# First states copied by ACT, half of the mixed differences on ACT and GpSimd, lower halves of the values subtracted from PSUM, in a two-layer RWKV kernel

## The chip, the cores and the metric

The kernel runs on one core of a Trainium2 chip. The metric is the device time of one execution in microseconds (us); lower is better. One execution was profiled.

Engines are called PE (the tensor engine; PEld is its weight load), DVE (VectorE), ACT (ScalarE), POOL (GpSimd) and SP (SyncE, which here only issues DMAs). Each works through its own instructions in order. SBUF is the working memory; PSUM is the memory that PE writes its products to, in banks of 512 float32 a partition.

## The reference, cut to what matters

The program is four layers one after the other on `x` of 16 sequences x 100 steps x 512 channels: an attention layer (0), an RWKV layer (1), an attention layer with a feed-forward part (2), and an RWKV layer (3) of the same form as layer 1. The change touches the RWKV layers alone. What one of them computes, shortened:

```python
xa = ln(x); sx = previous_step(xa) - xa                       # differences between steps
xxx = tanh((xa + sx * maa_x) @ maa_w1)                        # then five products with maa_w2
xm = xa[:, :, None] + sx[:, :, None] * (maa_stack + xxx)      # five mixes: k, w, v, r, g
w = exp(-exp(time_decay + tanh(xw @ td_w1) @ td_w2))
r, k, v = xr @ Wr.T, xk @ Wk.T, xv @ Wv.T;  g = silu(xg @ Wg.T)
def step(s, rkvw):                                            # 32 heads, state 16 x 16 each
    a = k[..., :, None] * v[..., None, :]
    out = einsum('bhi,bhij->bhj', r, u * a + s)
    return a + w[..., :, None] * s, out
out = group_norm(scan(step, s0, (r, k, v, w)))
x1 = x + (out * g) @ Wo.T
# then a channel part: layer norm, two mixes, Wfk, Wfr, Wfv
```

The state at the start, `s0`, comes from the context tensor.

## The kernel before

One RWKV layer is the function `rwkv(n, ...)`. The 16 sequences are taken in four groups `g` of four; a group's tiles hold 128 channels x `T` = 400 columns (4 sequences x 100 steps). The 512 channels are four chunks `c`; over the four groups there are 16 chunks `C`.

**Units.** The recurrence of one chunk is cut into 8 units of two value columns each, so a layer has `UNITS` = 128 units `u`. A unit needs `w` and `k` of its chunk, and the values `v` of two columns spread over the partitions:

- `spread(u)`: two PE matmuls write the spread values into `vbs[u % 2]`, one of two PSUM tiles of two banks each, shifted by one column. The values go through the PE as two float32r halves, `hi` and `lo` (`lo` = value minus `hi`), which `split` makes and which pass through DRAM and come back as the chunk's tile `xc`.
- `product(u)`: a DVE copy (128 x 8 elements) puts the first states, from `first_states[g]`, into the first column of each sequence, and a DVE product multiplies the other columns by `k` in place.
- `scan(u)`: two DVE scans over 400 columns make the states `a`; POOL multiplies them by `r`.
- `gather(p)`: for two units at once, PE sums the products into the PSUM bank `acc`. After a chunk's last one, `norm(C)` makes the group norm: ACT copies and squares, and two slots later `variance` takes one PE matmul, then an Ln and an Exp on ACT, each with a load of its function table.

**Slots.** The main loop runs over slots `u`. In each slot it calls `spread(u + 1)`, `product(u)`, `slots.begin()` (work put off to this slot, `variance` among it), `scan(u)`, `slots.end()` (late readers of PSUM banks), then the transfers and small steps of the chunk, and `gather` in every second slot. Then it fills the slot with `pieces`: the projections and mixes of a coming group, output products and the channel part of a finished one, each with a cost in us, until 2.85 us or a little less is used up.

**Banks.** The pieces use three PSUM banks in turn, `slots.bank()`. A reader that is put off with `slots.read_later(bank, fn)` is written at the end of the next slot, or earlier if its bank is wanted again.

**Mixes.** `mixed(fs, c)` makes one or two of the five products with `maa_w2` for chunk `c`. Its reader `read` is one DVE instruction, (product + `maa_stack`) x `sx`, from PSUM into a tile `tm` (a ring of four that other steps use too), and one POOL sum with `xa` into `xj[f]`, which the projections of `linear` read.

**Values.** `plain(2, "Wv", "v", co)` reads a value projection: ACT copies the bank to `v` and stores it, `split` makes `hi` on ACT from the bank, and, put off with `read_later`, `lo` on DVE from the tile `v` in SBUF and `hi`.

Every DVE, ACT, POOL and PE instruction of these steps is kept in the order in which the program text issues it (`InOrder`, whose line L89 most rows of the profile bear; PE's is L94). DMAs issued by SP are placed by the scheduler. Group 0's projections run before unit 0, at negative slots; the projections of groups 1 to 3 run beside the units.

Of the kernel before, what the change touches and what calls it, by code (L numbers as in the profile page):

```python
# [10 lines left out]
F32R = mybir.dt.float32r  # L11
BF16 = mybir.dt.bfloat16
U8 = mybir.dt.uint8
AF = mybir.ActivationFunctionType
ALU = mybir.AluOpType
# [3 lines left out]
NC = E // 128  # L19
G = 4  # L20
NG = B // G
T = G * L
# [15 lines left out]
def xattn_sequence(ctx: ExitStack, tc: tile.TileContext, d: dict, out: bass.AP):  # L38
# [52 lines left out]
    vector, scalar, gpsimd = InOrder(nc.vector), InOrder(nc.scalar), InOrder(nc.gpsimd)  # L91

    def mm(**kw):
        pin(nc.tensor.matmul(**kw))  # L94
# [606 lines left out]
    def rwkv(n, ws, small, first, next_weights, last):  # L701
# [6 lines left out]
        with ExitStack() as es:  # L708
# [9 lines left out]
            vec, w1, td1, gwb = (small[k] for k in ("vec", "w1", "td1", "gwb"))  # L718
# [29 lines left out]
            put, first_states, lower = {}, {}, {}  # L748
# [170 lines left out]
            def states(g):  # L919

                s0 = first_states[g] = two.tile([128, NC, G, 16], F32, tag="s0", name=f"s0_{n}_{g}")
                nc.sync.dma_start(out=s0, in_=d["s0"][:, :, g * G : (g + 1) * G, :])

            def projections(g, base):
# [6 lines left out]
                def store(t, c, tile):  # L931
                    (nc.sync if t in ("lo", "g") else scalar).dma_start(out=to[t][c], in_=tile)

                rows = [xb[g * G + i] for i in range(G)]
                st, xn, xj = {}, [], {}
# [85 lines left out]
                def mixed(fs, c):  # L1021

                    banks = []
                    for f in fs:
                        if c == 0:
                            xj[f] = two.tile([128, NC, T], F32, tag="xm", bufs=4, name=f"xj_{nm}_{f}")
                        banks.append(slots.bank())
                    for f, ps in zip(fs, banks):
                        cols = slice(c * 128, (c + 1) * 128)
                        mm(out=ps[:, :T], lhsT=w2[f][:, cols], rhs=zs[f], start=True, stop=True)  # L1030

                    def read(f, ps):
                        tm = two.tile([128, T], F32, tag="tm", bufs=4, name=f"tm_{nm}_{f}_{c}")
                        vector.scalar_tensor_tensor(
                            tm, ps[:, :T], vec[f"stack{f}"][:, c : c + 1], st["sx"][:, c, :], ALU.add, ALU.mult
                        )
                        gpsimd.tensor_tensor(steps(xj[f][:, c, :]), steps(tm), xa(c), ALU.add)

                    for f, ps in zip(fs, banks):
                        mixes[f].append(slots.read_later(ps, lambda f=f, ps=ps: read(f, ps)))  # L1040
# [10 lines left out]
                def plain(f, w, t, co):  # L1051
                    def read(ps):
                        out = stage(f"{t}_{nm}_{co}")
                        scalar.copy(out[:, :T], ps[:, :T])
                        store(t, co, out[:, :T])
                        if t == "v":
                            split(ps, out[:, :T])

                    def split(ps, v):

                        hi = stage(f"hi_{nm}_{co}")[:, :T]
                        scalar.copy(hi.bitcast(F32R), ps[:, :T])
                        store("hi", co, hi)

                        lo = stage(f"lo_{nm}_{co}")[:, :T]

                        def low():
                            vector.tensor_tensor(lo.bitcast(F32R), v, hi, ALU.subtract)
                            store("lo", co, lo)

                        lows[co] = slots.read_later(ps, low)

                    linear(f, ws[w], co, read, ("in", g, co if t == "r" else 0))
# [259 lines left out]
            vb4 = lambda u: vbs[u % 2][:, :, 1 : T + 1].rearrange("p i (b t) -> p i b t", t=L)  # L1333

            def spread(u):

                C, j = u // 8, 2 * (u % 8)
                for i in range(2):
# [2 lines left out]
                        start=True, stop=True,  # L1341
                    )

            def product(u):
                C, j = u // 8, 2 * (u % 8)
                g = C // NC
                vector.tensor_copy(
                    vb4(u)[:, :, :, 0], first_states[g][:, C % NC, :, j : j + 2].rearrange("p b i -> p i b")
                )
                p4 = vb4(u)[:, :, :, 1:L]  # L1350
                vector.tensor_tensor(
                    p4, p4,
                    steps(chunks[u // 8]["k"])[:, None, :, 0 : L - 1].to_broadcast([128, 2, G, L - 1]), ALU.mult,
                )
# [78 lines left out]
            UNITS, LEAD = 32 * NG, (36.0, 46.0, 42.0)  # L1433
            START = -19
            u, due, blended = START, 0.0, 0
            while u < UNITS + 6 or pieces or slots.due or slots.late:
                slots.now = u
                if u == UNITS + 2 and not last:
                    nws[""] = first_stats(f"a{n}", vector, gpsimd)
                if u == UNITS:  # L1440
                    for i in range(max(len(pieces) - 8, 0), len(pieces)):
                        pieces[i] = (pieces[i][0], u + 9, *pieces[i][2:])
                if u % 32 == 0 and 0 < u <= UNITS:
                    output(u // 32 - 1, u + 7)
                short = sum(p[0] for p in pieces) < LEAD[(len(put) == NG) + (blended > 0)]
                for g in range(NG):
                    if u == max(32 * g - 24, START):
                        states(g)
                    if u == max(32 * g - 4, START + 6):
                        centered(first_states[g].rearrange("p c b s -> p (c b) s"), 16, f"s{n}_{g}")  # L1450
                if u == START + 3:
                    centered(ws["Wv"].rearrange("p c (x s) -> p (c x) s", s=16), 128, f"w{n}")
                if u == START + 10:
                    ws["Wo"] = load_turned(d[f"L{n}_Wo"], f"l{n}_Wo")
                if u == START:
                    projections(0, u + 1)
                elif short and u > START + 10 and len(put) < NG:
                    wait = int(left(("mix", len(put) - 1, 4)) / 2.6) + 2
                    projections(len(put), u + (max(wait, 9) if u > 0 else 6))
                elif short and len(put) == NG and blended < NG:  # L1460
                    g = blended
                    if u >= 32 * g + 40 and not any(p[3] == ("wo", g) for p in pieces):
                        if g == 0:
                            cm.update(load(n, "Wfk", "Wfr", "Wfv"))
                        wait = max(int(left() / 2.6) - 5, int(left(("mix", NG - 1, 4)) / 2.6) + 1, int(left(("keys", g - 1)) / 2.6)) if u < UNITS else 0
                        channel_stream(g, u + max(wait, (3, 3, 3, 2)[g]), (1, 1, 1, 0)[g])
                        blended += 1
                if u >= UNITS and set(nws) <= {""} and not any(p[3] == ("wo", NG - 1) for p in pieces):
                    nws.update(next_weights())
                unit = 0 <= u < UNITS  # L1470
                if 0 <= u + 1 < UNITS:
                    spread(u + 1)
                if unit:
                    product(u)
                slots.begin()
                if unit:
                    scan(u)
                slots.end()
                C, at = u // 8 + 1, u % 8
                if 0 <= C < NC * NG:  # L1480
                    if at == 2:
                        enter(C)
                    elif at == 6:
                        bonus(C, 0)
                C = u // 8
                if 0 <= C < NC * NG and at == 0:
                    bonus(C, 1)
                if 0 <= C < NC * NG and at == 2:
                    bonus(C, 2)
                if 0 < C <= NC * NG and at == 4:  # L1490
                    gates(C - 1)
                if u % 2 and 0 <= (u - 3) // 2 < UNITS // 2:
                    gather((u - 3) // 2)

                due = min(due, 0.0) + (2.85 if 0 <= u < UNITS else 3.9)
                due -= 0.45 * (u % 2) + 0.7 * (at in (0, 2, 3)) if unit else 0.0
                for p in [p for p in pieces if p[0] == 0 and not callable(p[1]) and p[1] <= u]:
                    take(p)
                while due > 0:
                    p = following(u)  # L1500
                    if p is None:
                        break
                    due -= take(p)
                u += 1
# [360 lines left out]
    def load(layer, *names):  # L1865
        return {k: load_w(d[f"L{layer}_{k}"], f"l{layer}_{k}") for k in names}
# [80 lines left out]
```

## Time and profile before

| | us |
|---|---|
| median of 3 runs | 3128.99 (3123.95 to 3131.28) |
| profiled execution, its time | 3127.86 |
| profiled execution, its span | 3126.1 |

| engine | busy in the span, us | share | instructions |
|---|---|---|---|
| PE | 2858.8 | 91% | 16323 |
| DVE | 1675.5 | 54% | 3507 |
| ACT | 1308.6 | 42% | 2921 |
| POOL | 1159.3 | 37% | 953 |

The profile gives, for one execution, the busy time of each engine, also in 40 equal slices of the span (each digit is a share in tenths) and in any window; the granted clock of PE (`PEclk`, 1.00 is full); groups of instructions of one line, engine, operation and tile (`out<-in`, shapes, `x`count, then busy us, mean ns of one, then the engine's idle time just before them and what ended it); the waits (who waited for whom: us in total, times, longest us); a timeline (start us, duration us); and the chain of work that ended last. Buffer numbers are left out of tile names: `mm` is any of the three banks, `vb` either of the two spread tiles.

### The profile page before, as it was taken

The page shows a single profiled execution, that of the slowest core. Times are in us where ns is not written, and L with a number is a line of the kernel's source. Part 1 is how long each engine was busy: PE and PEld are TensorE (multiplying, and loading weights), DVE is VectorE, ACT ScalarE, POOL GpSimd, SP SyncE. Part 2 cuts the span into 40 slices and gives each one's busy share as a digit, 9 for nine tenths or more (in the row PEclk, how much of TensorE's full clock was granted, in tenths as well). Part 3 has the DMA queues.
Part 4 walks back from the last instruction along what each step waited for, and adds up shares of the span by engine and source line. Part 5 has one row for each costly group of instructions (what it writes and reads, how often), then busy time and mean ns, then how long its engine had stood idle before and what let it go on. Part 6 is the DMA issues. An engine that isn't in the chain of part 4 may idle for free. (4 is left out here: it accounts for less than half of the span.)

```text
span 3126.1 us, 44079 instructions
## 1 busy us (share of the span) xinstructions
PE 2858.8 (91%) x16323; PEld 1488.0 (48%) x16323; DVE 1675.5 (54%) x3507; ACT 1308.6 (42%) x2921; POOL 1159.3 (37%) x953
## 2 busy tenths in 40 slices
PE   6999999878889999989999999989999789999998
PEld 3555555534344444444555555455555344444444
DVE  2555556553989988433333333331000369998981
ACT  3777677753435355422222232221111335344553
POOL 0111111133777777412222111220000367787771
PEclk9999999989999999989999999999999889999999
DMA  6010101013224353230000001020002323324321
GB/s 196 24 34 24 34 24 37 3 39 116 80 77 129 96 161 87 71 88 21 21 22 21 21 21 34 28 71 11 11 11 62 101 63 106 109 76 155 105 60 56
DMA packets 139561, 195.93 MB, mean 63 GB/s; under 512 B 23974, under 2 KB 106854, under 8 KB 139346
## 3 DMA queue, kind: packets, MB, share of 16 engines
q1 hardware_dynamic: 116306, 160.34, 17.3%
q10 hardware_dynamic: 23040, 32.78, 2.9%
q8 instruction: 128, 2.10, 0.3%
q14 instruction: 87, 0.71, 0.1%
HBM read 117.16 MB, written 49.15 MB: 53 GB/s over the span
## 5 line engine op out<-in xcount | busy, mean ns | idle before, releaser
L89 POOL TENSOR_TENSOR a<-a,rc 128x800 f32<-128x800 f32 x256 | 487.8, 1908 | 175.8 <-DVE a L89 113.1
L89 DVE TENSOR_TENSOR_SCAN a<-wc,vb 128x400 f32<-128x400 f32 x512 | 477.4, 974 | 28.1 <-PE acc L94 2.2
L89 DVE CUSTOM_DVE_ANT_0 pr<-l_sc,mask 100x361 f32<-100x361 f32 x512 | 252.1, 529 | 148.7 <-PE l_sc L94 148.6
L89 ACT ACTIVATE pr<-pr,nm 100x361 f32<-100x361 f32 x512 | 301.2, 593 | 5.8 <-POOL sums L89 3.7
L89 DVE TENSOR_TENSOR vb<-vb,kc 128x792 f32<-128x792 f32 x256 | 253.8, 991 | 8.8
L97 PEld LDWEIGHTS l_pT<-ident,pr 100*121 100x121 f32 x1536 | 193.3, 186 | 104.3 <-issue 50.9
L1639 DVE CUSTOM_DVE_ANT_0 junk<-l2a_sc,mask 100x361 f32<-100x361 f32 x256 | 136.9, 535 | 182.5 <-PE l2a_sc L94 165.0
L94 PE MATMUL vb<-xc,sel 128*128 128x400 f32 x512 | 207.0, 487 | 18.0 <-DVE a L89 17.8
L97 PE MATMUL l_pT<-ident,pr 100*121 100x100 f32 x1536 | 216.4, 276 | 6.2 <-ACT pt L89 4.3
L1675 POOL TENSOR_TENSOR pa<-pt,pt 121x1600 f32<-121x1600 f32 x16 | 57.1, 3570 | 363.7 <-ACT pt L1670 363.7
L89 ACT COPY pt<-l_pT 121x400 f32<-121x400 f32 x256 | 125.1, 489 | 149.5 <-PE l_pT L97 148.5
L1860 DVE TENSOR_TENSOR x<-pb,x 100x512 f32<-100x512 f32 x16 | 12.6, 790 | 319.9 <-DMA pb<-po 310.1
L89 POOL TENSOR_TENSOR xj<-tm,ext 128x400 f32<-128x400 f32 x160 | 153.6, 981 | 80.1 <-DVE tm L89 59.8
L94 PE MATMUL v<-l_v_w,ct 128*121 128x512 f32 x384 | 177.0, 605 | 0.0
L75 PE MATMUL h<-yTb,l_fc 128*128 128x400 f32 x512 | 172.8, 499 | 0.6 <-ACT yTb L343 0.6
L94 PE MATMUL k<-ct,l_k_w 128*128 128x361 f32 x512 | 170.6, 476 | 0.0
L75 PE MATMUL p<-l_proj,h 128*128 128x512 f32 x384 | 165.5, 592 | 0.0
L89 POOL TENSOR_SCALAR ve<-mv 100x1 f32<-100x1 f32 x16 | 3.6, 224 | 409.8 <-DVE mv L89 409.8
L94 PEld LDWEIGHTS vb<-xc,sel 128*128 128x128 f32 x512 | 97.2, 198 | 109.5 <-issue 36.1
L94 PE MATMUL l_sc<-kz,qz 32*100 32x361 f32 x1024 | 112.6, 509 | 36.1 <-DVE nm L89 33.9
L89 DVE COPY pt<-l_pT 121x400 f32<-121x400 f32 x128 | 73.5, 574 | 132.1 <-PE l_pT L97 64.8
L75 PEld LDWEIGHTS h<-yTb,l_fc 128*128 128x128 f32 x512 | 96.9, 190 | 74.3 <-ACT yTb L343 2.5
(298 smaller groups left out, 5158.0 us busy)
## 6 DMA issues: line engine op xcount, KB each, us to landing
ct<-in_ctxT SPq DMA_DIRECT2D x32, 722.0 KB
dk<-k ACTq DMA_DIRECT2D x32, 200.0 KB
kc<-dk SPq DMA_DIRECT2D x32, 200.0 KB
dv<-v ACTq DMA_DIRECT2D x32, 200.0 KB
dhi<-hi ACTq DMA_DIRECT2D x32, 200.0 KB
dlo<-lo SPq DMA_DIRECT2D x32, 200.0 KB
vc<-dv SPq DMA_DIRECT2D x32, 200.0 KB
dw<-wd ACTq DMA_DIRECT2D x32, 200.0 KB
```

Of the source, the lines that this page charges most:

```text
L75: nc.tensor.matmul(out=ps, lhsT=lhs(c), rhs=rhs(c), start=(c == 0), stop=(c == n - 1))
L89: return lambda *args, **kw: tc.keep_in_program_order(op(*args, **kw))
L94: pin(nc.tensor.matmul(**kw))
L97: pin(nc.tensor.transpose(out, in_, ident))
L1639: nc.vector.tensor_tensor_reduce(out=junk, in0=ss[r][:L, :S2], in1=t["mask"], scale=-1.0, scalar=FLT_MAX, op0=ALU.add, op1=ALU.min, accum_ ...
L1675: nc.gpsimd.tensor_tensor(t["pa"], t["pt"][0], pt, ALU.add)
L1860: nc.vector.tensor_tensor(x, pb[:, i, :], x, ALU.add)
```

## The change

Three edits, all inside `rwkv`:

1. The copy of the first states leaves `product(u)` and DVE. A new function `begin_states(u)` does it on ACT, and the main loop calls it for unit u + 1 in slot u, after `slots.begin()`.
2. In `mixed`, for groups 1 to 3 and where f + c is odd, the one DVE instruction becomes an ACT activate (product + `maa_stack`, from PSUM into `tm`) and a POOL product with `sx` in place. That is 10 of the 20 mixes of a group, 30 of the 80 of a layer.
3. `lo` is subtracted from the PSUM bank instead of from the copy `v` in SBUF; it stays on DVE and stays put off.

```diff
                     def read(f, ps):
                         tm = two.tile([128, T], F32, tag="tm", bufs=4, name=f"tm_{nm}_{f}_{c}")
-                        vector.scalar_tensor_tensor(
-                            tm, ps[:, :T], vec[f"stack{f}"][:, c : c + 1], st["sx"][:, c, :], ALU.add, ALU.mult
-                        )
+                        if (f + c) % 2 and g:
+                            scalar.activation(tm, ps[:, :T], AF.Identity, bias=vec[f"stack{f}"][:, c : c + 1], scale=1.0)
+                            gpsimd.tensor_tensor(tm, tm, st["sx"][:, c, :], ALU.mult)
+                        else:
+                            vector.scalar_tensor_tensor(
+                                tm, ps[:, :T], vec[f"stack{f}"][:, c : c + 1], st["sx"][:, c, :], ALU.add, ALU.mult
+                            )
                         gpsimd.tensor_tensor(steps(xj[f][:, c, :]), steps(tm), xa(c), ALU.add)
...
-                            split(ps, out[:, :T])
+                            split(ps)
...
                         def low():
-                            vector.tensor_tensor(lo.bitcast(F32R), v, hi, ALU.subtract)
+                            vector.tensor_tensor(lo.bitcast(F32R), ps[:, :T], hi, ALU.subtract)
                             store("lo", co, lo)
...
+            def begin_states(u):
+
+                C, j = u // 8, 2 * (u % 8)
+                scalar.copy(
+                    vb4(u)[:, :, :, 0], first_states[C // NC][:, C % NC, :, j : j + 2].rearrange("p b i -> p i b")
+                )
+
             def product(u):
-                C, j = u // 8, 2 * (u % 8)
-                g = C // NC
-                vector.tensor_copy(
-                    vb4(u)[:, :, :, 0], first_states[g][:, C % NC, :, j : j + 2].rearrange("p b i -> p i b")
-                )
                 p4 = vb4(u)[:, :, :, 1:L]
                 vector.tensor_tensor(
...
                 if unit:
                     product(u)
                 slots.begin()
+                if 0 <= u + 1 < UNITS:
+                    begin_states(u + 1)
                 if unit:
                     scan(u)
                 slots.end()
```

In the built program the instructions of PE stand in the same order before and after.

More of the change, by code (lines that the diff above doesn't have):

```diff
@@ L1056, in read, with split @@
                         if t == "v":
-                            split(ps, out[:, :T])
-                    def split(ps, v):
+                            split(ps)
+                    def split(ps):
                         hi = stage(f"hi_{nm}_{co}")[:, :T]
```

## The prediction

> **What bounds the kernel now.** I read the page's 40 slices first, since the change touches only the two RWKV layers.
>
> ```profile
> PE   6999999878889999989999999989999789999998
> DVE  2555556553989988433333333331000369998981
> ACT  3777677753435355422222232221111335344553
> POOL 0111111133777777412222111220000367787771
> ```
>
> VectorE (DVE) is at 80 to 90% in two stretches alone, slices 11 to 16 and 34 to 39 (counted from 1): the 128 units of layer 1 and of layer 3. There the tensor engine (PE) is as full, while ACT has room. The table of busy time for the two stretches (the second is a near copy of the first):
>
> ```profile
> core 0: us, PE busy (x) PEld busy (x) DVE busy (x) ACT busy (x) POOL busy (x), PEclk, DMA share, GB/s
> 780.00:1290.00 510.00, 466.87 (x2058) 226.45 (x2058) 454.33 (x642) 232.04 (x416) 393.18 (x306) 0.96 0.33 100
> 2530.00:3045.00 515.00, 474.92 (x2076) 230.22 (x2077) 456.30 (x643) 232.30 (x417) 396.73 (x306) 0.94 0.31 96
> ```
>
> Per unit 4.0 us: DVE 3.55, PE 3.65, POOL 3.1, ACT 1.8. So PE has 43 us idle in the first stretch and 40 in the second. Beyond that only a fuller clock could help (0.96 and 0.94 granted). What DVE does there, by groups of the first stretch:
>
> ```profile
> L89 DVE TENSOR_TENSOR_SCAN a<-wc,vb 128x400 f32<-128x400 f32 x248 | 231.2, 974 | 14.5 <-PE acc L94 1.6 <-DVE vb L89 1.0 <-POOL a L89 0.9
> L89 DVE SCALAR_TENSOR_TENSOR tm<-mm,vec,sx 128x400 f32<-128x400 f32 x60 | 35.3, 620 | 5.9 <-PE mm L94 4.4 <-POOL xj L89 1.2
> L89 DVE COPY vb<-s 128x8 f32<-128x8 f32 x124 | 20.2, 163 | 19.0 <-PE vb L94 19.0
> L89 DVE TENSOR_TENSOR lo<-v,hi 128x400 fp32r<-128x400 f32 x12 | 16.3, 1354 | 3.6 <-ACT hi L89 3.3
> ```
>
> The last three rows are what the change touches. DVE waits for PE before the copies only 19 us in all, so most units are set by DVE. The waits between 800 and 1260 us say the same from PE's side (its weight load and its matmul wait for the reader of a PSUM bank):
>
> ```profile
> PEld mm L94 <- DVE tm L89: 21.5, 21, 2.2
> PE mm L94 <- DVE tm L89: 8.7, 10, 1.8
> ```
>
> **First states.** Removed from DVE: 256 copies of 0.163 us, 0.20 us from the copy's start to the product's: 128 x 0.20 = 25.6 us a layer. Added to ACT: as many 8-element copies. No row shows one; the nearest are ACT's accumulator reads (187 ns) and its 128x128 activate (268 ns): I take 0.2, between 0.16 (DVE's own) and 0.27. On ACT, with 278 us free in a stretch, 26 us of work is hidden. [...]
>
> The price is the wait. DVE's product of unit u+1 now waits for ACT's copy, and ACT works in order: the copy stands behind all that slot u's begin puts on ACT. Once in 8 units that is the group norm's Ln and Exp with two table loads:
>
> ```profile
> 1079.62 1.28 ACT L89 ACT_TABLE_LOAD   x1 [5.07 <-PE mm L94]
> 1080.92 0.59 ACT L89 ACTIVATE sq<-mm,eps 128x400 f32<-128x400 f32 x1
> 1081.53 1.28 ACT L89 ACT_TABLE_LOAD   x1
> 1082.82 0.54 ACT L89 ACTIVATE sq<-sq 128x400 f32<-128x400 f32 x1
> ```
> ```profile
> 1078.76 1.86 DVE L89 TENSOR_TENSOR_SCAN a<-wc,vb 128x400 f32<-128x400 f32 x2
> 1080.54 0.15 DVE L89 COPY vb<-s 128x8 f32<-128x8 f32 x1
> 1080.73 0.99 DVE L89 TENSOR_TENSOR vb<-vb,kc 128x792 f32<-128x792 f32 x1
> ```
>
> Here DVE copied at 1080.54; ACT is free at 1083.36, so with 0.3 us for copy and signal the product starts 2.9 us later than now, and behind it on DVE stand two scans and the bank readers (ox here) that PE waits for. I did this for all units: the end of the ACT instruction that stands ahead of the new copy (or of the spread's matmul, if later) plus 0.3 us, less the start of DVE's copy now. In layer 1 the 14 Ln/Exp slots are late by 38 us in sum: 20 in units 0 to 89, 18.5 in units 90 to 127. In 44 other slots it is late by 40 us in sum, mostly by under 1 us and where DVE waits for PE's spread anyway; the exceptions are the value projections, where ACT itself is full (1100 to 1120 us: up to 4 us late). Units 0 to 89 are set by DVE: I charge all 20. In units 90 to 127 PE is the fuller one (10.0 of 10 us in most windows) and the second vb buffer gives DVE a unit of slack: I charge a third, 6. Of the 40 I charge a quarter, 10. All of it charged would be 78, none 0: kept for the range.
>
> **Mixed differences.** In groups 1 to 3, 10 of 20 a group: 30 of 60 leave DVE in each layer. Start to start one costs 0.57 us (two in 1.15): 30 x 0.57 = 17 us. ACT gains 30 activates with a bias from PSUM, of 0.68 us as `ext` has them: 20 us, hidden in its 278, though in its queue. GpSimd (POOL) gains 30 products of two SBUF tensors, as `xj` at 0.98: 29 us on 393 of 510. The xj sums behind them come later by up to 4 us in a run of four pairs, and the ring of four `tm` tiles empties later (one DVE wait of 1.2 us on it now). PE's gathers have a median 4.2 us between the end of POOL's a and their start, which covers that; I price POOL at 0, at worst 4 us for each of 3 runs of pairs, 12 a layer. [...]
>
> **Lower halves.** `lo` takes 1.354 us mean, 0.549 at best, 3.915 at worst, against 0.552 for `rk`, the same shape with one side in PSUM. 12 x 0.80 = 9.6 us a layer (the four of group 0 come before the units, off DVE's full stretch). The price: PE's next use of the bank now waits for DVE's `lo`, which ran after the next unit's scans, where before it waited only for ACT's `hi`. PE's waits for `tm`, the like reader, are at most 30.2 us on the 53 of that window: 0.57 each, so 12 x 0.57 = 6.8 us; from 0 (DVE early) to 2.2 each, 26.
>
> **Queues.** PE's order is the same. SyncE's has the same 962 transfers with some dlo, rc, gc and s issues exchanged; operands are fetched some six units (24 us) ahead, so 0, and at worst one landing of 4 to 6 us as the chain shows them, per group.
>
> **The sum, a layer:** 25.6 + 17 + 9.6 = 52 off DVE; 20 + 6 + 10 + 6.8 = 43 back; 9 us remain. Two layers: 18 us. The profiled execution took 3127.86 (span 3126.1), beside a median of 3128.99: 3127.9 - 18 = **3110**.
>
> **Rivals.** *ACT's queue becomes the bound (slower).* One mechanism: the product stands behind the Ln/Exp pair and its table loads. All 38 late us count, because DVE's bank readers stand behind the product and PE waits for them, and half of the other 40: 58 + 6.8 against 52, and with POOL's 12: +25 a layer, 3178; with POOL at 0, +13 a layer, 3154. It decides once a chunk of 8 units loses more than 52/16 = 3.3 us. For it: the example above, where PE already waits for `ox` behind that very product. Against it: the double vb buffer. *DVE is relieved and PE becomes the bound:* PE's idle time falls from 43 to about 10 us a layer, and the clock dips (0.57 at 1030 to 1040, after a PE wait of 1.6 for DVE's reader of `g`) partly go: -70, 3058. Against: ACT's table loads stay. *Nothing:* both sums meet within 6 us, 3128.
>
> **Chances.** Forecast, a modest gain, 0.37 (3085 to 3121); PE-bound 0.15; nothing 0.10; ACT's queue 0.38. 0.2% (6 us) is about what a measurement of this kernel can tell from no change. Faster 0.52, same 0.10, slower 0.38. The range runs from near the PE-bound case, 3064, to just past the rival without POOL, 3160.
>
> **What would show it.** Right: DVE busy falls by about 50 us in each stretch; `lo` near 0.55 us; no copies on DVE; DVE's idle before `vb<-vb` becomes large, 20 to 60 us a layer, released by ACT's copy, most of it once in 8 units behind `sq`; ACT's copies near 0.2 us. PE's waits for `tm` shrink, some for `lo` appear. Wrong: if these ACT waits stay under 10 us a layer, the gain is the larger one; if PE's waits for DVE's readers grow, or its granted clock falls below 0.94, it is the slower one; if DVE waits for POOL's xj, my zero for POOL was.

## The result, and the profile after

The changed kernel took 3231.15 us (median of 4 runs, 3228.87 to 3231.89) against 3126.47 us (4 runs, 3123.92 to 3131.28) for the kernel before on the same chip: a ratio of 1.0332 [1.0314, 1.035], slower by 104 us. The forecast was 3110, the range ended at 3160. The profiled execution has a span of 3227.0 us. From here on a difference is (ratio - 1) x 3130 us, because the kernel before moved by some us from chip to chip.

The 40 slices of the page, PE, DVE, ACT, POOL, as those of before were shown:

```profile
PE   6999899877889799989999999899998888888998
...
DVE  2555555644777677523343333321001377776871
ACT  3777677733535355422232323211111344435543
POOL 0111111144787776512212111220001388786761
```

DVE went from 8 and 9 tenths to 7 in the two stretches, as wanted, but PE fell with it. The same work now needs longer windows. In the table of busy time for the two stretches, the 560 us from 780 hold 2055 PE instructions, where 510 us held 2058 before:

```profile
core 0: us, PE busy (x) PEld busy (x) DVE busy (x) ACT busy (x) POOL busy (x), PEclk, DMA share, GB/s
780.00:1340.00 560.00, 485.08 (x2055) 235.19 (x2053) 409.56 (x486) 262.47 (x567) 421.72 (x336) 0.92 0.29 91
2580.00:3140.00 560.00, 483.31 (x2057) 233.92 (x2058) 412.84 (x488) 261.93 (x568) 425.23 (x336) 0.92 0.28 88
```

Read the first row against the row of before (510 us, PE 466.87, DVE 454.33, clock 0.96). DVE has 45 us less to do. PE has 75 us idle instead of 43, which is 32 of the 50 us; the other 18 are the same matmuls taking 485 us instead of 467 at a clock of 0.92. From the start of the first unit's product to the end of the last unit's, the trace gives 570 and 565 us for the two layers against 519 and 516, so 100 of the 101 us that the span grew lie there.

The groups of that window show what came of each edit (the last part is idle time before the group, and who ended it):

```profile
L89 DVE TENSOR_TENSOR vb<-vb,kc 128x792 f32<-128x792 f32 x124 | 122.0, 984 | 96.6 <-ACT vb L89 96.0
...
L89 POOL TENSOR_TENSOR tm<-tm,sx 128x400 f32<-128x400 f32 x30 | 31.0, 1034 | 7.1 <-ACT tm L89 7.0
...
L89 ACT COPY vb<-s 128x8 f32<-128x8 f32 x123 | 20.5, 169 | 101.1 <-PE vb L94 70.2 <-issue 16.0 <-DVE vb L89 2.9
...
L89 ACT ACTIVATE tm<-mm,vec 128x400 f32<-128x400 f32 x30 | 17.7, 590 | 4.6 <-POOL xj L89 2.3 <-PE mm L94 2.3
...
L89 DVE TENSOR_TENSOR lo<-mm,hi 128x400 fp32r<-128x400 f32 x12 | 6.8, 570 | 11.6 <-ACT hi L89 11.6
```

The instructions themselves are cheap: ACT's copy 0.169 us, its mix 0.59, POOL's product 1.03, `lo` 0.57 in place of 1.35. What is dear is the first row's idle time: 96 us in which DVE waits for ACT's copy, where before it waited 19 us for PE ahead of its own copy. The waits between 800 and 1310 us (who waited for whom: us, times, longest) add PE's side:

```profile
DVE vb L89 <- ACT vb L89: 88.3, 49, 7.7
...
PEld mm L94 <- POOL xj L89: 21.5, 9, 4.6
...
PEld mm L94 <- ACT tm L89: 16.5, 12, 3.4
...
PE mm L94 <- POOL xj L89: 15.2, 8, 3.9
...
PEld mm L94 <- DVE lo L89: 11.3, 9, 3.0
```

Before, between 780 and 1290 us, the weight load waited 4.0 us for POOL's `xj`, never for `lo`, and it had no ACT `tm` to wait for. Ten microseconds of the timeline (start, duration) show two of these side by side:

```profile
923.59 1.28 ACT L89 ACT_TABLE_LOAD   x1
...
926.09 0.60 ACT L89 ACTIVATE sq<-mm,eps 128x400 f32<-128x400 f32 x1 [1.21 <-PE mm L94]
926.59 1.03 POOL L89 TENSOR_TENSOR tm<-tm,sx 128x400 f32<-128x400 f32 x1
926.70 1.28 ACT L89 ACT_TABLE_LOAD   x1
927.70 0.97 POOL L89 TENSOR_TENSOR xj<-tm,ext 128x400 f32<-128x400 f32 x1
928.00 0.54 ACT L89 ACTIVATE sq<-sq 128x400 f32<-128x400 f32 x1
928.44 0.16 ACT L89 COPY vb<-s 128x8 f32<-128x8 f32 x1
928.62 1.03 POOL L89 TENSOR_TENSOR tm<-tm,sx 128x400 f32<-128x400 f32 x1
928.63 0.99 DVE L89 TENSOR_TENSOR vb<-vb,kc 128x792 f32<-128x792 f32 x1 [1.30 <-ACT vb L89]
...
929.73 1.88 POOL L89 TENSOR_TENSOR xj<-tm,ext 128x400 f32<-128x400 f32 x2
...
931.67 0.67 PE L94 MATMUL mm<-xj,td_w 128*64 128x400 f32 x1 [2.06 <-POOL xj L89]
```

ACT loads a table, waits for PE's variance, loads the other table, and only then makes the copy that DVE's product needs. Beside it POOL makes product, sum, product, sum, sum in 5 us, and the projection `td_w` starts 0.06 us after the last sum.

### The profile page after: what moved, and what is told of

Same layout as the page of the kernel before. It is cut to its first block, busy times and chain, and to the rows that moved or that the text cites. A ratio compares the mean times of both kernels' runs of the same rounds, so it can differ in the third digit from the quotient of the medians.

```text
span 3227.0 us, 44370 instructions
## 1 busy us (share of the span) xinstructions
PE 2887.7 (89%) x16323; PEld 1502.5 (47%) x16323; DVE 1587.7 (49%) x3191; ACT 1372.8 (43%) x3237; POOL 1217.5 (38%) x1013
## 5 line engine op out<-in xcount | busy, mean ns | idle before, releaser
L94 PE MATMUL vb<-xc,sel 128*128 128x400 f32 x512 | 215.4, 505 | 27.4 <-DVE a L89 20.0
L89 ACT COPY vb<-s 128x8 f32<-128x8 f32 x256 | 42.7, 169 | 210.3 <-PE vb L94 155.7
```

Source lines behind the costliest of these rows:

```text
L89: return lambda *args, **kw: tc.keep_in_program_order(op(*args, **kw))
```

## The experiments

Fifteen kernels, each against the kernel before on its own chip.

| run | what is in it | ratio [95%] | difference, us |
|---|---|---|---|
| e1_states | edit 1 | 1.0139 [1.0122, 1.0156] | +44 |
| e2_mixes | edit 2 | 1.0082 [1.0067, 1.0097] | +26 |
| e3_lo | edit 3 | 1.0017 [1.0004, 1.003] | +5 |
| e4_states_early | edit 1, copy ahead of `begin` | 1.0026 [1.0012, 1.004] | +8 |
| e5_no_copy | before, no copies | 0.9929 [0.9905, 0.9953] | -22 |
| e6_states_no_tables | edit 1, no table loads | 0.9999 [0.9985, 1.0014] | 0 |
| e7_before_no_tables | before, no table loads | 1.0004 [0.9989, 1.0018] | +1 |
| e8_mixes_no_product | edit 2, no POOL product | 0.9973 [0.9959, 0.9988] | -8 |
| e9_states_mixes | edits 1 and 2 | 1.0316 [1.0299, 1.0332] | +99 |
| e10_mixes_lo | edits 2 and 3 | 1.0077 [1.0062, 1.0092] | +24 |
| e11_whole_early | all, copy ahead of `begin` | 1.0131 [1.0112, 1.015] | +41 |
| e12_mixes_late | edit 2 on 18 mixes of 30 | 1.0058 [1.0043, 1.0073] | +18 |
| e13_states_mixes_no_product | edits 1 and 2, no POOL product | 1.0199 [1.0168, 1.023] | +62 |
| e14_whole_no_tables | all, no table loads | 1.0169 [1.014, 1.0199] | +53 |
| e15_states_but_fifth | edit 1, one unit in 8 as before | 1.0021 [1.0004, 1.0038] | +7 |

### The three edits one by one

**e1_states** holds edit 1 of the diff alone.

> The first edit alone: first states copied by ACT a slot ahead, after the slot's begin; mixes and lower halves as before. Theory A (DVE's product waits behind ACT's queue, above all behind the group norm's Ln and Exp with their table loads): most of the 103 us of the whole change is here, 60 to 110 us over the kernel before, and DVE idles 70 to 100 us a layer before its product, about 42 of it behind sq. Theory B (the mixes' work on GpSimd and the later xj sums cost it): this one is within 25 us of before.

Measured: +44 us, less than theory A's 60 and more than theory B's 25. The product's group between 780 and 1290 us:

```profile
L89 DVE TENSOR_TENSOR vb<-vb,kc 128x792 f32<-128x792 f32 x119 | 116.9, 982 | 67.5 <-ACT vb L89 67.1
```

67 us of idle time for 19 before. By the ACT instruction ahead of each late copy, 35 us of layer 1's wait (73 over all its units) stand behind `sq`, the Ln and Exp pair, 9 behind `zh`, the rest in small pieces.

**e2_mixes** holds edit 2 alone.

> The second edit alone: half of the mixed differences on ACT and GpSimd. Theory A: within 25 us of before, as 17 us less on DVE a layer stand against PE's waits for xj. Theory B: 60 us or more over before, with PE's waits for POOL's xj at some 35 us a layer as in the changed kernel (3.6 before).

Measured: +26 us, again between the two theories. PE's waits between 780 and 1290 us:

```profile
PEld mm L94 <- POOL xj L89: 19.1, 10, 4.6
...
PEld mm L94 <- ACT tm L89: 14.2, 10, 3.6
...
PE mm L94 <- POOL xj L89: 11.5, 7, 3.9
```

The projections wait for POOL's sums up to 4.6 us at a time.

**e3_lo** holds edit 3 alone.

> The third edit alone: lower halves subtracted from PSUM. Both theories: 0 to 20 us under before; lo at 0.55 to 0.57 us each where it was 1.35, some waits of PE for lo. If it is over before by more than 10 us, the longer hold of the bank costs more than the 9.6 us a layer saved on DVE.

Measured: +5 us, hardly more than can be told from nothing, but not the gain that both theories expected. `lo` takes 0.57 us, 8 to 9 us a layer leave DVE, and these waits appear in the same window:

```profile
PEld mm L94 <- DVE lo L89: 15.5, 8, 4.2
...
DVE lo L89 <- ACT hi L89: 11.5, 7, 2.7
PE mm L94 <- DVE lo L89: 11.3, 8, 3.6
```

The bank that ACT alone used to free is now held until DVE comes round, and DVE waits for `hi` longer (3.3 before). What was saved came back.

The trace of before shows when `lo` was long from SBUF. Sixteen of its 32 started while a POOL product of 400 or 800 columns was running, and each of those ended 0.43 to 0.44 us after a POOL product that it overlapped, after 0.65 to 3.9 us in all; the other sixteen took 0.55 to 0.58 us. Read from PSUM, in e3 and in the changed kernel, all 32 take that, beside POOL or not.

### Where edit 1 loses

**e4_states_early** puts the copy ahead of the slot's begin, so that the Ln and Exp stand behind it.

```diff
                     product(u)
-                slots.begin()
                 if 0 <= u + 1 < UNITS:
                     begin_states(u + 1)
+                slots.begin()
```

> The first edit alone, but the copy for the next unit is issued ahead of the slot's begin instead of after it, so that ACT makes it before the Ln and Exp. Theory A: the 42 us a layer behind sq go, and the kernel is at least 50 us faster than the first edit as it was; 10 us under to 30 us over before. Theory B: no different from the first edit as it was. If it is the signal between the engines that costs (a hop from PE over ACT to DVE in each unit), it stays 50 us or more over before.

Measured: +8 us; the new place takes back 35 of the 44, where theory A asked for 50.

```profile
DVE vb L89 <- ACT vb L89: 42.4, 27, 4.7
```

The wait falls from 67 us to 42. Behind `sq` only 3 us are left in layer 1; 22 now stand behind ACT's `r`, `wd` and `k`, and 9 behind `zh` as before.

**e5_no_copy** leaves the copies out and fills the first column of both tiles once.

```diff
+            for vb in vbs:
+                vector.tensor_copy(vb[:, :, 1], heads8[:, 0:2])
...
-                vector.tensor_copy(
-                    vb4(u)[:, :, :, 0], first_states[g][:, C % NC, :, j : j + 2].rearrange("p b i -> p i b")
-                )
```

> The kernel before with the 256 copies of the first states left out (the first step of each sequence then gets no state): DVE has 0.20 us less in each unit, and nothing is put anywhere else. If DVE sets the pace of the units, as the prediction read it: 30 to 50 us under before. If the units run at PE's pace and DVE only seems full (rival): within 15 us of before. This tells what the first edit could have brought at best.

Measured: -22 us [-30, -15], between the two readings' 30 to 50 and 15. This is all that edit 1 could ever give: 51 us of DVE's time bring 22. By the starts of the products, units 0 to 89 take 365 us in both layers instead of 375 and 376, and units 90 to 127 take 143 and 139 instead of 145 and 140.

**e6_states_no_tables** is edit 1 with the Ln and Exp made Identity; between 780 and 1290 us no table is loaded then, where e1 has 30 loads of 1.28 us; **e7_before_no_tables** is the same on the kernel before, as a control.

```diff
-                    scalar.activation(sq, ps[:, :T], AF.Ln, bias=eps, scale=1.0)
-                    scalar.activation(sq, sq, AF.Exp, scale=-0.5)
+                    scalar.activation(sq, ps[:, :T], AF.Identity, bias=eps, scale=1.0)
+                    scalar.activation(sq, sq, AF.Identity, scale=-0.5)
```

> The first edit alone, with the group norm's Ln and Exp replaced by two Identity activates (another function is computed, with the same number of instructions), so that no table is loaded in the units: ACT is free 2.6 us earlier in that slot. If the table loads ahead of the copy are the cost: at least 25 us under the first edit as it was, and DVE's wait behind sq falls from 36 us a layer to under 12. If only the extra hop counts: no more under it than the next kernel is under before.

> The control to the one ahead of it: the kernel before with the same two Identity activates instead of Ln and Exp, so without table loads in the units. Expected within 10 us of before, as ACT is not full there and DVE does not wait for it; if it is 30 us or more under before, the table loads cost time in any case and the pair must be compared by difference.

Measured: 0 us and +1 us. In the kernel before, the table loads cost nothing, since DVE waited for nothing behind them. With the copy on ACT they cost 44; DVE's wait behind `sq`, 35 us in e1, is 10 in layer 1 without them. And without them the way over ACT still eats the 22 us of e5. DVE's wait ahead of the product, 25 us for PE in e5, is here:

```profile
DVE vb L89 <- ACT vb L89: 47.4, 31, 3.4
```

**e15_states_but_fifth** leaves the copy on DVE in the one unit in eight that stood behind the Ln and Exp.

```diff
-                scalar.copy(
+                (vector.tensor_copy if u % 8 == 4 else scalar.copy)(
...
+                if u % 8 == 4:
+                    begin_states(u)
...
-                if 0 <= u + 1 < UNITS:
+                if 0 <= u + 1 < UNITS and (u + 1) % 8 != 4:
```

> The first edit alone, but the unit whose copy would stand behind the Ln and Exp (the fifth of each eight) keeps its copy on DVE: seven of eight copies leave DVE and no copy waits for a table load. Copies left out brought 20 us, the hop over ACT without table loads cost those 20 again: 10 us under to 10 over before. This is the version of the first edit that could beat the kernel before.

Measured: +7 us [1, 12]. It takes away the loss, as e6 does, and like e6 has no gain. No version of edit 1 tried here beats the kernel before.

### Where edit 2 loses

**e8_mixes_no_product** leaves out POOL's product.

```diff
-                            gpsimd.tensor_tensor(tm, tm, st["sx"][:, c, :], ALU.mult)
+                            pass
```

> The second edit alone without GpSimd's product (the difference is then not multiplied by sx in those 60 mixes): ACT reads the bank, GpSimd makes only the sum as before. If GpSimd's extra 30 us a layer and the later xj sums cost the 26 us of the second edit: this is within 8 us of before or under it, and PE's waits for xj are near 4 us a layer again. If it is ACT's place in the queue as a reader of the banks: it stays 15 us or more over before.

Measured: -8 us, so POOL's product is worth 34 us of e2's time, for 60 instructions of 1.04 us. The waits of the same window:

```profile
PEld mm L94 <- ACT tm L89: 12.7, 9, 3.6
...
PEld mm L94 <- POOL xj L89: 6.3, 5, 3.2
```

The wait for `xj` is near its 4.0 of before; the wait for ACT's reading of the bank stays. From the first product to the last scan, the two layers take 21 and 17 us more in e2 than in e8. Ten us of each are idle time of PE, 8 and 9 of them ended by `xj`; the other 11 and 8 are the same matmuls taking longer, at a lower clock: 0.92 in e2 and 0.95 in e8 between 780 and 1290 us, 0.95 and 0.97 between 2580 and 3140.

**e12_mixes_late** moves only the mixes with f over 1, 18 of 30 a layer, and so spares the run at a group's start.

```diff
-                        if (f + c) % 2 and g:
+                        if (f + c) % 2 and g and f > 1:
```

> The second edit alone, kept to the products 2, 3 and 4 (18 mixes a layer on ACT and GpSimd instead of 30): the runs of products 0 and 1 stay on DVE, whose eight sums come one after another on GpSimd and are wanted at once by the decay's projection. If GpSimd's product costs where its sums are wanted at once: within 8 us of before or under it. If it costs everywhere: 12 to 18 us over before.

Measured: +18 us. That is 0.50 us for each of 36 moved mixes, against 0.43 for each of 60 in e2: the cost is spread over all of them, and not the first run's. PE's waits for `xj`, between 780 and 1290 us, are back near e8's here (6.3 and 3.4 us there):

```profile
PEld mm L94 <- POOL xj L89: 7.7, 5, 2.6
...
PE mm L94 <- POOL xj L89: 4.9, 4, 2.0
```

So these waits are a part of what the mixes cost, and not the whole of it.

### The edits together

**e9_states_mixes** holds edits 1 and 2, **e10_mixes_lo** edits 2 and 3.

> The first and the second edit together, without the third. One by one they cost 44 and 26 us; the three alone make 75 of the whole change's 103. If the missing 28 us come from the first two sharing ACT's queue (ACT's readers of tm wait for GpSimd and the next unit's copy stands behind them): 85 to 100 us over before. If they add up: 65 to 75.

> The second and the third edit together, without the first. Added up: 31 us over before. If the missing 28 us come from these two (both make PE wait for its banks): 45 to 60.

Measured: +99 and +24 us. Edit 3 adds nothing to edit 2, and 5 us to the other two (99 to 104). Edits 1 and 2 together cost 30 us more than 44 and 26.

**e13_states_mixes_no_product** takes POOL's product out of e9, with e8's diff.

> The first and the second edit together, without GpSimd's product (those mixes are then not multiplied by sx). Measured so far: the two together 97 us over before, the first alone 44, the second alone 26, the second without the product 9 under. If the 27 us that the two cost beyond their sum come from GpSimd's product, which makes PE wait and lowers its clock: about 35 us over before. If they come from ACT's longer queue ahead of the copy: 55 us or more over before.

Measured: +62 us [53, 72], 26 more than e1 and e8 together (44 - 8), with some 12 either way. The product costs 37 us here and 34 alone, so the excess isn't the product's; what edits 1 and 2 still share is ACT's queue, with copies and mixes in it. DVE's wait for the copy doesn't show how: between 780 and 1290 us it is 67 us in e1, and in e9, then in e13:

```profile
DVE vb L89 <- ACT vb L89: 86.9, 45, 7.7
```
```profile
DVE vb L89 <- ACT vb L89: 70.2, 43, 5.2
```

Most of the 20 us by which DVE waits longer in e9 than in e1 go with the product, while the excess stays.

**e11_whole_early** is the whole change with the copy ahead of the slot's begin (e4's diff); **e14_whole_no_tables** is the whole change without table loads (e6's diff).

> The whole change, but with the copy for the next unit issued ahead of the slot's begin. With the first edit alone that gave back 35 of 44 us. If the table loads ahead of the copy are the largest single cost in the whole too: 35 to 65 us under the whole change, so 40 to 70 over before. If the whole is by then set by GpSimd's xj: within 20 us of the whole change.

> The whole change with Identity in place of the group norm's Ln and Exp (another function), so without table loads in the units. With the first edit alone that took all 44 us. If the table loads are behind the 27 us beyond the sum as well, what is left is the second edit's 26 and a little: 20 to 40 us over before. If the first two edits hold each other up without them too: 45 us or more.

Measured: +41 and +53 us; the table loads are 51 of the whole's 104. With the copy ahead of the begin hardly anything exceeds the single edits (8 + 26 + 5 = 39, with some 10 either way). Without table loads 22 us of excess are left (53 against 0 + 26 + 5 = 31, with some 12 either way), of 29 with them. So the place of the copy in ACT's queue makes the excess, and the table loads don't explain it alone. Which of ACT's other instructions does, and by whose wait, was not separated.

## Why the prediction was wrong

All figures here are us a layer, half of a run's difference; plus is slower.

| term | forecast | measured | from |
|---|---|---|---|
| copies leave DVE | -25.6 | -11 | e5 |
| copy on ACT, slots without Ln and Exp | +10 | +11 | e6 against e5 |
| copy behind Ln and Exp | +26 | +22 | e1 against e6 |
| mixes leave DVE, ACT's part | -17 | -4 | e8 |
| POOL's product | 0 | +17 | e2 against e8 |
| `lo` from PSUM | -2.8 | +3 | e3 |
| edits 1 and 2 together | not priced | +15 | e9 against e1, e2 |
| sum | -9 | +53 | after: +52 |

The measured column is made of differences between runs, so that it adds up says little; the last row checks only that edit 3 adds to e9 what it costs alone. A run's difference is good to about 5 us either way, to 7 for e5 and 10 for e13 and e14.

**The first step that failed is "most units are set by DVE".** Every microsecond taken off DVE was counted as one off the time, 52 a layer, in all units alike. e5 shows 43 in 100. In units 0 to 89, which the prediction called DVE's, 18 us off DVE bring 9 and 10; in units 90 to 127, where it had read PE as the fuller one and yet counted the saving whole, 8 us bring 1. In these stretches PE was as full as DVE (467 and 454 of 510), and what DVE gained, PE took only in part: with the copies gone, PE's busy time in 510 us rises from 467 to 477, and DVE's wait for PE ahead of the product from 19 to 25. What keeps PE from taking more (it is still idle for 37 us a layer in e5, after 48 and 44) was not separated. That DVE seldom waits for PE had been read as DVE's bound, though PE's 43 us of idle time stood beside it, less than the 52 us of savings that were counted in full.

**The prices of the Ln and Exp and of the other slots held in their sum, in part by luck.** 36 were charged, 33 measured. How late the copies would be was well foreseen: 38 us behind the pair and 40 elsewhere, and in e1 DVE waits 35 and 37. But the shares charged did not hold: from e6 to e1, units 0 to 89 lose 13 us a layer (20 charged for the pair) and units 90 to 127 lose 8 (6 charged). e6 also keeps two activates ahead of the copy, with 10 us of wait behind them, so the two rows of the table don't part exactly where the forecast did. The rival's mechanism is real, but it is 22 of 52, and the rival too counted 52 us of savings; so it came to 3154 to 3178, and the time was 3231.

**POOL's zero failed, and in part by its reader.** The prediction asked whether the later sums would delay the gathers, found 4.2 us of slack there, and stopped. But `xj` is read by the projections, which come in the next pieces; in the stretch of the timeline they have no slack: PE starts 0.06 us behind POOL's end. Idle time of PE that `xj` ends is 8 to 9 of the 17 us (e8); most of the others are matmuls at the lower clock (between 780 and 1290 us 0.92 in e2, 0.95 in e8). The sign named in advance, DVE waiting for `xj`, came at 4.6 us ahead of its mixes; the one that told more was PE's.

**The mixes' own saving was also too large**, 4 for 17. It isn't ACT's price (0.59 us, 0.68 charged), nor the bank: PE's weight load waits for a reader of `tm` 19.9 us in e8 (ACT's 12.7 and DVE's 7.2), and 23.6 us before. By e5's rate the 17 would be worth 7; what takes the other 3 was not separated.

**`lo`** did shrink to 0.57, and the wait for the bank was the named price, but taken near its low end (6.8 in a range of 0 to 26).

**Not seen at all:** edits 1 and 2 were priced alone. Both put work into ACT's one queue, and what they cost beyond their sum goes when the copy is issued ahead of the slot's begin (e11); by which wait it comes stays open. ACT is busy 262 of 560 us, so it looks free, and it is the order more than the amount that costs: e4 has e1's work in another order and loses 8 us instead of 44.

**The signs.** Right: DVE's 45 us less, `lo` at 0.57, the copy's 0.169 us (0.2 taken), and PE's shorter waits for DVE's `tm`. Wrong: DVE's wait for the copies is 96 us and not 20 to 60, and only 42 of it stands behind `sq`, not most. The sign given for the slower case, a clock below 0.94, is there: 0.92 in both stretches. DVE's scans and products kept their times beside POOL's added products: 973 and 984 ns, after 974 and 991.

## What to carry to other kernels

Price a saving on a busy engine by what the next engine can take of it: leave the instruction out and time that first (here 51 us off DVE were worth 22), since moving it will hardly bring more. An engine with half its time free is no free place for a step that another engine waits for; look up what stands ahead of it in that in-order queue, table loads above all (44 us here, e1 against e6), and price edits that share a queue together. When a step becomes later, follow its output to the instruction that reads it, and take the slack there and nowhere else. When PE has to wait more, read its granted clock as well as its idle time: of the 21 us that layer 1 takes longer in e2 than in e8, 10 are idle time and 11 the same matmuls at a lower clock (next section).

## What the runs showed of the hardware

PE's granted clock did not follow PE's idle time alone. Between 780 and 1290 us, e1, then e2, then e9:

```profile
780.00:1290.00 510.00, 452.16 (x1929) 219.19 (x1922) 414.99 (x496) 239.78 (x523) 377.66 (x296) 0.95 0.32 99
```
```profile
780.00:1290.00 510.00, 460.98 (x1939) 223.11 (x1938) 424.57 (x592) 240.98 (x435) 411.99 (x328) 0.92 0.32 99
```
```profile
780.00:1290.00 510.00, 439.89 (x1825) 212.44 (x1825) 380.41 (x444) 241.36 (x525) 386.97 (x306) 0.91 0.31 96
```

e2 has about as many matmuls as e1, less idle time on PE, and a lower clock. In this stretch all kernels with POOL's product and 30 mixes show 0.91 to 0.94, those without 0.94 to 0.96, and e12, with 18 mixes, 0.94; between 2580 and 3140 us it is 0.92, 0.92 and 0.95 in the changed kernel, e9 and e2, and 0.95 to 0.97 in the kernel before, e1, e3 to e6, e8 and e13.

The changed kernel's ten microseconds above end with a fall of the clock. In the 4 us from 928 PE is busy for 1.22 us, waits for `xj` and has a clock of 1.00; in the 6 us behind them the clock is 0.50:

```profile
928.00:932.00 4.00, 1.22 (x6) 0.40 (x8) 2.86 (x3) 0.60 (x2) 3.92 (x5) 1.00 0.00 0
932.00:938.00 6.00, 5.50 (x13) 2.81 (x10) 2.83 (x4) 2.28 (x5) 6.00 (x5) 0.50 0.01 3
```

A lowered clock is more frequent after the change. In windows of 10 us, it is below 0.90 in 8 of 51 from 780 us on and in 8 of 52 from 2530 on before; in the changed kernel in 19 of 56 from 780 on and in 18 of 56 from 2580 on. If the time of the matmuls goes inversely with the mean clock, the 467 us at 0.96 become 487 at 0.92, an estimate; 485 were measured. With POOL's product left out, e8's clock is 0.95 and 0.97 where e2's is 0.92 and 0.95, so a part of the lower clock goes with that product and with the waits for `xj` (the weight load's are 6.3 us in e8 and 19.1 in e2, between 780 and 1290 us). What makes the clock fall in one wait and not in another was not shown.
